# Block-attention residual on one core: where VectorE's row products take their factor from

## The chip, the cores and the metric

The kernel runs on one core of a Trainium2 chip. The metric is the device time of one execution in microseconds (us). The core has TensorE (PE in the profile; PEld is its weight load), VectorE (DVE), ScalarE (ACT), GpSimd (POOL) and SyncE (SP), whose queue issues almost all DMAs.

## What is computed

The input x is 8 x 512 x 1024 in float32, with a conditioning vector q and two 1024 x 1024 weights. For each batch entry, with H = 1024 and EPS = 1e-6:

```
block_repr = inputs.reshape(B, 8, 64, H).sum(axis=2)
keys = block_repr @ Wk.T;  keys = keys / sqrt(mean(keys^2) + EPS) * rms_weight
attn = softmax(keys @ q)
proj = (attn @ block_repr) @ Wo.T          # one row for each batch entry
y = inputs + proj
out = inputs + (y - mean(y)) / sqrt(var(y) + EPS) * ln_gamma + ln_beta
```

So every row of x needs the attention of its whole batch entry first, then a layer norm, and the original row is added at the end. Writing rs for a row's 1/std, mu for its mean and g for gamma, the result is y(1 + g rs) less a term of rank few: -proj - mu rs g + beta.

## The kernel before

**Tiling.** The 4096 rows are 32 "rows" of 128 partitions x 1024, numbered k = 0 to 31, two to a tile of 1 MB. The eight entries are worked on in three groups (`GROUPS`) of 2, 4 and 2 entries: k = 0 to 7, 8 to 23 and 24 to 31. Wk and Wo are loaded, turned on TensorE and kept.

**Attention of a group** (`attention`, L480). Sums over blocks go into `bs` on TensorE (L508); for tiles marked in `SUMS` with G or V, GpSimd or VectorE first adds the tile's two rows into `two` (L500), which halves TensorE's work. Then come keys, softmax, V (L534), and the projection spread over all partitions into a PSUM tile `pb` (L622). A bf16 table `tab` holds the rank-few term, cut into bf16 pieces by `split` (L411, L415).

**Unit and row** (`unit`, `pairs`, `pair`, `row`). For each row VectorE makes y = x + pb with its sum (L676) and ScalarE squares it (L683). A unit of 2 or 4 rows (`UNITS`) shares a `std` step on GpSimd (L692, L693) and a `sp` step (L715 to L719) that cuts mean x 1/std into three bf16 pieces in `stat`. Per tile TensorE turns these over into `pl` (L740), which ScalarE or VectorE (`TURN`) copies to `lt` (L745, L747). The matmul of `lt` with `tab` (L780) puts the rank-few term into a PSUM tile `C`. How the row is multiplied by (1 + g rs) is set by its letter in `KINDS`:

- A: ScalarE writes the factor to `A` (L776), GpSimd multiplies (L795), VectorE adds C (L826).
- P: as A, but TensorE adds the row into C by an identity matmul (L784) and ScalarE copies C out (L814).
- G: GpSimd multiplies by gamma into `A` (L797), TensorE puts the row into C (L784), VectorE does A x rs + C (L819).
- D: ScalarE writes the factor into C (L776), VectorE multiplies (L788) and, once TensorE has overwritten C, adds it (L826).
- E: VectorE alone: a reciprocal of rs (L790), (gamma + 1/rs) x row (L791, three operands in SBUF), then that x rs + C (L819).

Then the tile is stored (L763; the last tile in three parts, L758).

**Buffers and order.** `SLOTS` gives 13 x tiles, two `A`, and in PSUM three `big` tiles (4 KB each; used by `pb` and by every C) and two `s`. `A` and C are handed out in order of k. The order on each engine is a planner's: `Plan.order` takes, on each engine, the ready step with the lowest number in `RANK`, with assumed durations. The result is a fixed program for each engine's in-order queue. `EVAC` says which engine copies the turned weights and three small tiles of each group; where the plan leaves TensorE idle, filler matmuls (L859) are put in.

Of the kernel before, what the change touches and what calls it, by code (L numbers as in the profile page):

```python
# [20 lines left out]
SLOTS = {"x": 13, "A": 2, "big": 3, "s": 2, "lt": 2, "pr": 1, "tab": 2, "ts": 1, "blkT": 1,  # L21
# [3 lines left out]
SUMS = "PPVPGGPVPPPPPPPP"  # L25
EVAC = "ADAAAAAAAAADADADADAAAAADAAAD"
TURN = "ADDAAAAAAAAAAAAA"
FILL = (0.5, 0.3, 0.28)
KINDS = "GEDAAAPPGGEEAPAEPEPPGPPEEEEPEAAE"
UNITS = [[(1, "P"), (1, "P"), (1, "P"), (1, "P")], [(1, "P"), (1, "P"), (1, "P"), (1, "P"), (2, "P"), (2, "P")], [(2, "P"), (1, "P"), (1, "P")]]  # L30
# [6 lines left out]
5 33 6 31 28 16 21 30 34 26 25 7 0 11 1 4 9 3 10 2 14 13 17 19 12 15 46 55 67 18 68 37 70 79 175  # L37
205 93 214 20 22 27 24 23 8 38 40 45 63 35 39 29 36 41 43 44 62 66 74 52 73 51 65 53 72 64 78 77 92
86 89 90 100 49 60 69 71 76 42 47 32 48 57 61 56 58 54 50 75 81 80 85 91 82 95 83 87 98 96 94 99
106 101 104 111 117 121 124 109 107 113 154 122 132 133 136 115 108 137 153 131 140 145 161 134 135  # L40
127 156 142 146 150 167 155 162 173 172 160 171 158 177 181 119 128 114 123 176 143 163 159 165 179
130 184 174 187 203 189 192 138 88 110 116 152 191 197 195 185 208 196 220 231 188 217 207 232 216
235 97 102 105 59 120 84 118 103 125 170 129 139 141 144 148 147 151 149 168 169 166 190 180 183
182 164 178 186 126 112 157 198 204 201 234 226 202 206 200 212 223 265 199 233 218 211 242 250 225
213 276 248 270 221 237 193 194 274 280 241 260 239 254 268 249 258 275 289 215 224 228 251 294 298
259 278 264 312 266 295 272 308 245 256 300 307 229 257 222 243 299 219 244 283 293 316 291 284 310
271 263 319 227 240 292 303 287 297 269 279 330 338 320 317 311 343 334 329 350 315 335 340 345 321
318 322 351 324 342 352 327 357 333 348 354 358 305 314 313 353 288 309 210 285 370 383 360 363 378
355 367 376 349 423 365 369 381 391 361 368 374 379 380 387 398 328 373 331 404 209 230 236 238 255
247 261 253 267 246 252 302 296 273 306 304 301 281 277 282 290 286 262 325 341 323 337 388 396 336  # L50
346 356 364 326 339 344 371 372 386 392 397 332 347 395 400 401 394 414 399 407 382 409 393 390 362
410 412 417 420 366 385 377 384 389 405 403 406 436 416 424 402 411 418 415 428 359 408 375 413 419
421 425 426 422 438 429 434 427 430 431 432 437 435 433
# [117 lines left out]
def block_attn_resid_kernel(  # L171
# [25 lines left out]
    def flat(t):  # L197
        return t.rearrange("p a b -> p (a b)")
# [30 lines left out]
    ONES, MU = 12, 15  # L229
# [11 lines left out]
    b_w = Buf("A", [P, 5, P], F32, "wide")  # L241
# [6 lines left out]
    stat = {g: fixed([P, ROOM, 32], f"stat{g}", BF16) for g in sizes}  # L248
# [6 lines left out]
    inv = fixed([P, 4 * B], "inv")  # L255
# [35 lines left out]
    def c_small():  # L291
        pool.memset(eps_t, EPS)
        pool.memset(half_t[:, :1], -0.5)
        w = T(b_w)
        pool.tensor_copy(w[:, 0:4, :], row_of(GR).unsqueeze(2).to_broadcast([P, 4, P]))
        pool.tensor_copy(w[:, 4, :].rearrange("p (j m) -> p j m", j=4), row_of(0).unsqueeze(2).to_broadcast([P, 4, 32]))

# [45 lines left out]
    sums_ok = plan.add("c_sums", "DVE", 2.8, c_sums, [first])  # L343
# [3 lines left out]
    c_f = {g: plan.add(f"c_far{g}", "POOL", 0.3, lambda g=g: c_far(g), [sums_ok]) for g in sizes}  # L347
    c_p = {g: plan.add(f"c_pick{g}", "POOL", 2.4 if g < 4 else 2.8, lambda g=g: c_pick(g), [sums_ok]) for g in sizes}
    c_sp = {g: plan.add(f"c_spread{g}", "POOL", 0.5, lambda g=g: c_spread(g), [sums_ok]) for g in spread}
    c_st = {g: plan.add(f"c_stat{g}", "POOL", 1.0, lambda g=g: c_stat(g), [sums_ok]) for g in sizes}  # L350
# [68 lines left out]


# [242 lines left out]
    def unit(G, tiles, how):  # L663
        n, g = G["n"], G["g"]
        add = plan.add
        NU = RT * len(tiles)
        k0 = G["first"] + RT * tiles[0]
        sums = fixed([P, 5, NU], f"sum{k0}")
        at = lambda i: (xt[n, tiles[i // RT]][0], i % RT)
        X = lambda i: T(at(i)[0])[:, at(i)[1], :]  # L670
        sq, ys = [], []
        for i in range(NU):
            xb, ld = xt[n, tiles[i // RT]]
            y = add(
                f"y{k0 + i}", "DVE", 1.15,
                lambda i=i: nc.vector.scalar_tensor_tensor(  # L676
                    X(i), X(i), 1.0, flat(T(G["pb"])), ALU.mult, ALU.add, accum_out=sums[:, 0, i : i + 1]
                ), [ld, *G["pb_ok"]], [xb, G["pb"]],
            )
            ys.append(y)  # L680
            sq.append(add(
                f"sq{k0 + i}", "ACT", 1.27,
                lambda i=i: nc.scalar.activation(  # L683
                    junk, X(i), AF.Square, bias=sums[:, 0, i : i + 1], scale=-float(H),
                    accum_out=sums[:, 1, i : i + 1], saturate=False,
                ), [y], [xb],
            ))

        def std():
            v = sums  # L690
            if how == "P":
                pool.tensor_scalar(v[:, 2, :], v[:, 1, :], 1.0 / H**3, EPS, ALU.mult, ALU.add)  # L692
                pool.tensor_tensor(v[:, 4, :], v[:, 2, :], half_t[:, :NU], ALU.pow)  # L693
            else:
                nc.scalar.activation(v[:, 2, :], v[:, 1, :], AF.Ln, bias=eps_t, scale=1.0 / H**3)
                nc.scalar.activation(v[:, 4, :], v[:, 2, :], AF.Exp, scale=-0.5)

        if how == "P":
            rs = add(f"std{k0}", "POOL", {2: 0.96, 4: 1.28, 8: 1.9}[NU], std, [*sq, small], [])
        else:  # L700
            rs = add(f"std{k0}", "ACT", 0.45, std, [*sq, small], [])
        pairs(G, tiles, sums, ys, rs)

    def pairs(G, tiles, sums, ys, rs):
        n, g = G["n"], G["g"]
        NU = RT * len(tiles)
        k0 = G["first"] + RT * tiles[0]
        r0 = RT * tiles[0] % ROOM
        st = stat[g][:, r0 : r0 + NU, :]

        def pieces():

            at = lambda i: st[:, :, MU + 3 * i : MU + 3 * i + 3]
            wide = sums[:, 3, :].unsqueeze(2).to_broadcast([P, NU, 3])
            pool.tensor_tensor(sums[:, 3, :], sums[:, 0, :], sums[:, 4, :], ALU.mult)  # L715
            pool.tensor_copy(at(0), wide)  # L716
            pool.tensor_tensor(sums[:, 3, :], sums[:, 3, :], at(0)[:, :, 0], ALU.subtract)
            pool.tensor_copy(at(1), wide)
            pool.tensor_tensor(at(2), wide, at(1), ALU.subtract)  # L719

        before = [last_use.get((g, r0 + r)) for r in range(0, NU, RT)]
        a = plan.add(f"sp{k0}", "POOL", 1.36, pieces, [rs, c_st[g], *before], [])
        for t in tiles:
            r = RT * (t - tiles[0])
            last_use[g, r0 + r] = pair(G, t, sums, r, ys, rs, st[:, r : r + RT], a)

    def pair(G, t, sums, o, ys, rs, st, a):
# [23 lines left out]
        fin = [row(G, t, r, kinds[r], X, xb, sums[:, 4, o + r : o + r + 1], rs, lt, lt_ok, seen(r), C[r], A[r]) for r in range(RT)]  # L751
# [15 lines left out]
    def row(G, t, r, kind, X, xb, scale, rs, lt, lt_ok, seen, C, A):  # L767
# [18 lines left out]
        def product():  # L786
            if kind == "D":
                nc.vector.tensor_tensor(X(r), X(r), flat(T(C)), ALU.mult)  # L788
                return
            nc.vector.reciprocal(inv[:, k : k + 1], scale)  # L790
            nc.vector.scalar_tensor_tensor(X(r), gam, inv[:, k : k + 1], X(r), ALU.add, ALU.mult)  # L791
# [7 lines left out]
        elif kind == "D":  # L799
            a = add(f"A{k}", "ACT", 1.05, lambda: factor(flat(T(C))), [rs, gam_ok], [C])  # L800
            m = add(f"m{k}", "DVE", 1.15, product, [a], [C, xb])
            need.append(m)
        else:
            m = add(f"m{k}", "DVE", 1.3, product, [rs, gam_ok], [xb])
        c = add(f"C{k}", "PE", 0.38, lambda: outer(T(G["tab"]), kind != "G", kind != "P"), need, [C, lt, G["tab"]])
        if kind == "P":
            m = add(f"I{k}", "PE", 1.84, lambda: whole(False, True), [m, c], [C, xb])
        halves = k == S * B // P - 1
        ends = []
        for tag, cut in (("fa", slice(0, H // 2)), ("fb", slice(H // 2, H))) if halves else (("f", slice(0, H)),):  # L810
            if kind == "P":
# [4 lines left out]
            elif kind in "GE":  # L816
# [3 lines left out]
                        X(r)[:, cut], (at_A() if kind == "G" else X(r))[:, cut], scale, flat(T(C))[:, cut], ALU.mult, ALU.add  # L820
                    ), [c, m], [C, xb, *([A] if kind == "G" else [])],
# [74 lines left out]
```

## Time and profile before

| | |
|---|---|
| median of 3 runs | 149.99 us (149.7 to 150.47) |
| profiled execution: own time | 150.32 us |
| its span in the profile | 148.4 us, so 1.92 us lie around it |
| mean granted TensorE clock | 0.933 |
| busy: PE, DVE, ACT, POOL | 118.7, 103.5, 90.2, 94.3 us |
| first y of each group (L676) | 44.51, 70.43, 103.55 us |
| last VectorE instruction ends | 144.1 us |

Times within the execution count from the start of the span. A group of instructions is named by line, engine, operation and tiles, with its count, its busy time and the mean of one in ns. On VectorE one instruction often starts some 0.07 us before the one ahead is counted as finished; the "pitch", from start to start in an unbroken run, is what an instruction really takes of the engine.

### The profile page before, as it was taken

How to read it: one execution, taken by the hardware profiler on the slowest of the kernel's cores; microseconds unless marked ns; L12 is line 12 of the kernel's file. 1: busy time of each engine (PE TensorE's matmuls, PEld its weight loads, DVE VectorE, ACT ScalarE, POOL GpSimd, SP SyncE). 2: the span in 40 equal slices, each digit the busy share in tenths (PEclk: the TensorE clock that was granted, in tenths of full speed). 3: DMA queues.
4: the chain of work that ended last, by engine and by line, in shares of the span. 5: the costliest groups of instructions: out<-in, count | busy, mean ns of one | idle time of the engine just before them, and what ended most of it. 6: DMA issues, size and time to landing. Idle time of an engine off the chain costs nothing.

```text
span 148.4 us, 3151 instructions
## 1 busy us (share of the span) xinstructions
PE 118.7 (80%) x1222; PEld 72.5 (49%) x1222; DVE 103.5 (70%) x168; ACT 90.2 (61%) x148; POOL 94.3 (64%) x155
## 2 busy tenths in 40 slices
PE   4999959999988948999999869987978577299300
PEld 4999818888764513455543433553423123064100
DVE  4113003016439997687999999989999999946980
ACT  0319413565306968856799977899869698463200
POOL 8950000000057687899998689969999898997600
PEclk9999999999999996899999987999999999857965
DMA  5999999999999991549999207660706606660983
GB/s 168 402 430 422 417 387 407 402 413 421 419 422 415 417 382 42 221 119 338 426 395 404 86 0 287 283 283 0 287 0 283 283 0 283 283 249 35 377 329 143
DMA packets 7662, 42.15 MB, mean 284 GB/s; under 512 B 720, under 2 KB 736, under 8 KB 3680
## 3 DMA queue, kind: packets, MB, share of 16 engines
q1 hardware_dynamic: 7616, 41.95, 69.9%
q8 instruction: 9, 0.15, 0.4%
q14 instruction: 5, 0.04, 0.1%
q10 hardware_dynamic: 32, 0.02, 0.0%
HBM read 25.18 MB, written 16.78 MB: 283 GB/s over the span
## 4 chain that ended last, share of the span: by engine, by line
DVE 21%; PE 14%; issue 8%; ACT 8%; POOL 3%; DVEq 1%; POOLq 0%; ACTq 0%
DVE x L676 9%; DVE x L791 4%; ACT junk L683 4%; PE C L784 4%; PE keys L534 3%; DVE x L819 3%; PE V L534 3%; DVE x L826 2%; PE C L780 2%; ACT A L776 1%; PE pl L859 1%; POOL sum L693 1%; DVE ptab L415 1%; POOL stat L716 1%; PE pb L622 1%
## 5 line engine op out<-in xcount | busy, mean ns | idle before, releaser
L683 ACT ACTIVATE junk<-x,sum 128x1024 fp8e5<-128x1024 f32 x32 | 36.7, 1148 | 10.2 <-DVE x L676 8.3
L795 POOL TENSOR_TENSOR x<-x,A 128x1024 f32<-128x1024 f32 x16 | 38.5, 2429 | 1.0 <-ACT A L776 1.0
L676 DVE SCALAR_TENSOR_TENSOR x<-x,pb 128x1024 f32<-128x1024 f32 x32 | 37.6, 1214 | 0.9 <-PE pb L622 0.8
L784 PE MATMUL C<-x,ident 128*128 128x512 f32 x52 | 26.6, 642 | 0.5 <-POOL x L795 0.3
L500 POOL TENSOR_TENSOR two<-x 128x1024 f32<-128x1024 f32 x2 | 4.7, 2362 | 33.7 <-DMA x<-in_x_dram 32.9
L776 ACT ACTIVATE A<-gam,sum 128x1024 f32<-128x1024 f32 x16 | 18.2, 1147 | 2.7 <-POOL x L795 1.3
L791 DVE SCALAR_TENSOR_TENSOR x<-gam,inv,x 128x1024 f32<-128x1024 f32 x11 | 17.8, 1621 | 0.6
L443 PE MATMUL pt<-ident,w 128*128 128x128 f32 x128 | 15.6, 275 | 1.1 <-DMA w<-in_L_cond_Wk_dram 0.4
L784 PEld LDWEIGHTS C<-x,ident 128*128 128x128 f32 x52 | 9.6, 200 | 12.3 <-issue 9.0
L819 DVE SCALAR_TENSOR_TENSOR x<-x,sum,C 128x1024 f32<-128x1024 f32 (+1 forms) x12 | 14.1, 1186 | 2.0 <-PE C L780 1.9
L443 PEld LDWEIGHTS pt<-ident,w 128*128 128x128 f32 x128 | 13.9, 141 | 2.9 <-issue 1.4
L534 PE MATMUL keys<-wkT,blkT 128*32 128x128 f32 (+1 forms) x256 | 14.5, 372 | 0.0
L693 POOL TENSOR_TENSOR sum<-sum,half_t 128x2 f32<-128x2 f32 (+1 forms) x13 | 13.0, 1001 | 1.1
L508 PE MATMUL bs<-x,blk 128*32 128x256 f32 x192 | 12.0, 382 | 1.9 <-DMA x<-in_x_dram 1.9
L780 PE MATMUL C<-tab,lt 32*128 32x512 bf16 x64 | 8.5, 404 | 4.7 <-DVE x L819 2.0
L534 PE MATMUL V<-woT,blkT 128*32 128x128 f32 (+1 forms) x256 | 11.8, 328 | 0.0
L814 ACT COPY x<-C 128x1024 f32<-128x1024 f32 x9 | 8.9, 1004 | 4.0 <-POOL sum L693 3.6
L826 DVE TENSOR_TENSOR x<-x,C 128x1024 f32<-128x1024 f32 x8 | 9.6, 1214 | 1.2 <-POOL stat L716 1.2
L797 POOL TENSOR_TENSOR A<-x,gam 128x1024 f32<-128x1024 f32 x4 | 9.5, 2374 | 1.1 <-ACT junk L683 1.1
L534 PEld LDWEIGHTS keys<-wkT,blkT 128*32 128x32 f32 x256 | 7.7, 122 | 4.6 <-issue 2.9
L740 PE MATMUL pl<-identb,stat 128*32 128x128 bf16 x64 | 4.0, 237 | 6.3 <-POOL stat L719 4.3
L508 PEld LDWEIGHTS bs<-x,blk 128*32 128x32 f32 x192 | 5.5, 109 | 7.0 <-DMA x<-in_x_dram 2.8
(116 smaller groups left out, 168.6 us busy)
## 6 DMA issues: line engine op xcount, KB each, us to landing
x<-in_x_dram SPq DMA_DIRECT2D x16, 1024.0 KB, 10.5
out_dram<-x SPq DMA_DIRECT2D x15, 1024.0 KB, 3.9
w<-in_L_cond_Wk_dram SPq DMA_DIRECT2D x3, 1024.0 KB, 7.8
w<-in_L_cond_Wo_dram SPq DMA_DIRECT2D x3, 1024.0 KB, 15.7
w<-in_L_cond_Wk_dram SPq DMA_DIRECT2D x2, 512.0 KB, 3.2
w<-in_L_cond_Wo_dram SPq DMA_DIRECT2D x2, 512.0 KB, 16.5
out_dram<-x SPq DMA_DIRECT2D x2, 256.0 KB, 2.0
out_dram<-x SPq DMA_DIRECT2D x1, 512.0 KB, 2.6
```

Of the source, the lines that this page charges most:

```text
L443: nc.tensor.transpose(T(pt)[:, c, r * P : (r + 1) * P], T(sb)[:, r, bass.ts(4 * h4 + c, P)], ident)
L508: nc.tensor.matmul(T(bs)[32 * j : 32 * j + 32, :], blk[g], part()[:, bass.ts(j, QU)], start=(t == 0 and r == 0), stop=(t == nt - 1 and r = ...
L534: nc.tensor.matmul(dst[32 * j : 32 * j + 32, lo:hi], T(blkT)[:, c % 2, c // 2, :], wT[:, c, j * QU + lo : j * QU + hi], start=(c == 0), st ...
L676: lambda i=i: nc.vector.scalar_tensor_tensor(X(i), X(i), 1.0, flat(T(G["pb"])), ALU.mult, ALU.add, accum_out=sums[:, 0, i : i + 1]), [ld, ...
L683: lambda i=i: nc.scalar.activation(junk, X(i), AF.Square, bias=sums[:, 0, i : i + 1], scale=-float(H), accum_out=sums[:, 1, i : i + 1], sa ...
L693: pool.tensor_tensor(v[:, 4, :], v[:, 2, :], half_t[:, :NU], ALU.pow)
L776: nc.scalar.activation(out, gam, AF.Identity, bias=1.0, scale=scale)
L784: nc.tensor.matmul(T(C)[:, h, :], ident, X(r)[:, bass.ts(h, 2 * QU)], start=start, stop=stop)
L791: nc.vector.scalar_tensor_tensor(X(r), gam, inv[:, k : k + 1], X(r), ALU.add, ALU.mult)
L795: m = add(f"m{k}", "POOL", 2.37, lambda: pool.tensor_tensor(X(r), X(r), at_A(), ALU.mult), [a], [A, xb])
L819: lambda cut=cut: nc.vector.scalar_tensor_tensor(X(r)[:, cut], (at_A() if kind == "G" else X(r))[:, cut], scale, flat(T(C))[:, cut], ALU.m ...
L826: lambda cut=cut: nc.vector.tensor_tensor(X(r)[:, cut], X(r)[:, cut], flat(T(C))[:, cut], ALU.add),
```

## The change

No row is of kind E any more. Two kinds are new. In kind F TensorE writes g x rs into C by a matmul of `lt` with a new constant table `rise` (gamma rows in bf16 pieces) and VectorE multiplies the row by (C + 1); the rest is as in D. In kind R the product is F's and the end is P's (identity matmul, copy by ScalarE). So that `lt` can carry rs, rs too is cut in three pieces: the `sp` step does both numbers at once, with six instructions in place of five. `A` gets a third buffer. The kinds by group, the tiles added up ahead, the engines of copies, the units and the whole order change as well:

| | before | after |
|---|---|---|
| kinds, k = 0 to 7 | GEDAAAPP | GFADAAAP |
| k = 8 to 23 | GGEEAPAE PEPPGPPE | GGFFRGPA PFPAFFGP |
| k = 24 to 31 | EEEPEAAE | APDFPAFA |
| SUMS by tile | PPVP GGPVPPPP PPPP | PPGP GPPGPGPP GPPP |
| rows per unit | 2 2 2 2, 2 2 2 2 4 4, 4 2 2 | 2 2 2 2, 2 2 4 4 4, 4 4 |
| weight copies by DVE | 3 | 7 |
| `blkT`, `bss` by group | ADA, AAA | DAA, DAA |
| `lt` copies by DVE (tiles) | 1, 2 | 0, 1, 13, 15 |

```diff
-SLOTS = {"x": 13, "A": 2, "big": 3, "s": 2, "lt": 2, "pr": 1, "tab": 2, "ts": 1, "blkT": 1,
+SLOTS = {"x": 13, "A": 3, "big": 3, "s": 2, "lt": 2, "pr": 1, "tab": 2, "ts": 1, "blkT": 1,
...
-    stat = {g: fixed([P, ROOM, 32], f"stat{g}", BF16) for g in sizes}
+    stat = {g: fixed([P, ROOM, 33], f"stat{g}", BF16) for g in sizes}
+    rise = fixed([P, 2 * QU], "rise", BF16)
...
+        pool.memset(w[:, 6:8, :], 0.0)
+        for k in range(2):
+            v = w[:, 6 + k, :].rearrange("p (r i m) -> p r i m", r=2, i=2)
+            spot(v, RS, 8, k, GR)
...
+    b_r = buf("s", [P, 2, QU], "prise")
+    def rise_rows():
+        for k in range(2):
+            nc.tensor.matmul(T(b_r)[:, k, :], T(b_w)[:, 6 + k, :], gbq, start=True, stop=True)
+    pr_ok = plan.add("prise", "PE", 1.1, rise_rows, [vec, small], [b_r, b_w])
+    ri_ok = split(b_r, lambda: rise, "r", [pr_ok], [])
...
-            pool.tensor_tensor(sums[:, 3, :], sums[:, 0, :], sums[:, 4, :], ALU.mult)
-            pool.tensor_copy(at(0), wide)
-            pool.tensor_tensor(sums[:, 3, :], sums[:, 3, :], at(0)[:, :, 0], ALU.subtract)
-            pool.tensor_copy(at(1), wide)
-            pool.tensor_tensor(at(2), wide, at(1), ALU.subtract)
+            pool.tensor_tensor(own_rs(sums, 0), sums[:, 0, :], own_rs(sums, 1), ALU.mult)
+            pool.tensor_copy(at(0, 3), wide(3))
+            pool.tensor_tensor(cut(5), cut(3), at(0, 1)[:, :, :, 0], ALU.subtract)
+            pool.tensor_copy(at(3, 3), wide(5))
+            pool.tensor_tensor(cut(5), cut(5), at(3, 1)[:, :, :, 0], ALU.subtract)
+            pool.tensor_copy(at(6, 3), wide(5))
...
-                return
-            nc.vector.reciprocal(inv[:, k : k + 1], scale)
-            nc.vector.scalar_tensor_tensor(X(r), gam, inv[:, k : k + 1], X(r), ALU.add, ALU.mult)
+            else:
+                nc.vector.scalar_tensor_tensor(X(r), flat(T(C)), 1.0, X(r), ALU.add, ALU.mult)
...
+            else:
+                a = add(f"B{k}", "PE", 0.4, lambda: outer(rise), [lt_ok, ri_ok], [C, lt])
             m = add(f"m{k}", "DVE", 1.15, product, [a], [C, xb])
             need.append(m)
-        else:
-            m = add(f"m{k}", "DVE", 1.3, product, [rs, gam_ok], [xb])
...
-        if kind == "P":
+        if kind in "PR":
             m = add(f"I{k}", "PE", 1.84, lambda: whole(False, True), [m, c], [C, xb])
```

All numbers of `RANK` are new, and some of the planner's assumed durations.

## The prediction on record

> **What bounds the kernel now.** First the table of busy time by stretches. Its columns are the length, then PE, PEld, DVE, ACT and POOL busy with counts, the granted clock, the DMA share and GB/s:
>
> ```profile
> 44.50:70.40 25.90, 22.50 (x286) 11.17 (x286) 22.54 (x38) 18.97 (x32) 21.59 (x35) 0.93 0.70 276
> 70.40:144.10 73.70, 56.85 (x410) 27.11 (x410) 69.20 (x98) 54.86 (x93) 62.16 (x79) 0.92 0.56 228
> ```
>
> From 70.4 us, where the second group's first y starts, to the end of the last VectorE instruction, VectorE is busy for 69.2 of 73.7 us; DMA has slack. GpSimd has 62.2, yet little of the rest is idle: its small instructions leave some 0.07 us between them. Before 70.4 the second group's attention sets the pace (x tiles landing, sums, keys, V, all on DMA and TensorE), so a faster VectorE there mostly waits longer. I count gains from 70.4 on.
>
> Next the groups of instructions with forms kept apart (busy us and mean ns after the bar, then idle before):
>
> ```profile
> L795 POOL TENSOR_TENSOR x<-x,A 128x1024 f32<-128x1024 f32 x16 | 38.5, 2429 | 1.0 <-ACT A L776 1.0
> L676 DVE SCALAR_TENSOR_TENSOR x<-x,pb 128x1024 f32<-128x1024 f32 x32 | 37.6, 1214 | 0.9 <-PE pb L622 0.8
> L791 DVE SCALAR_TENSOR_TENSOR x<-gam,inv,x 128x1024 f32<-128x1024 f32 x11 | 17.8, 1621 | 0.6
> L819 DVE SCALAR_TENSOR_TENSOR x<-x,sum,C 128x1024 f32<-128x1024 f32 x10 | 12.7, 1274 | 1.9 <-PE C L780 1.9
> L826 DVE TENSOR_TENSOR x<-x,C 128x1024 f32<-128x1024 f32 x8 | 9.6, 1214 | 1.2 <-POOL stat L716 1.2
> ```
>
> The E product (L791) has a mean of 1621 ns, but its shortest is 1283 and its median 1285. So the eleven hold 17.8 - 11 x 1.285 = 3.7 us of something else. The timeline says what; DVE's lines, then POOL's (start, duration):
>
> ```profile
> 104.88 3.14 DVE L791 SCALAR_TENSOR_TENSOR x<-gam,inv,x 128x1024 f32<-128x1024 f32 x1
> ...
> 126.91 1.28 DVE L791 SCALAR_TENSOR_TENSOR x<-gam,inv,x 128x1024 f32<-128x1024 f32 x1
> ```
> ```profile
> 102.25 7.99 POOL L795 TENSOR_TENSOR x<-x,A 128x1024 f32<-128x1024 f32 x3
> ...
> 125.10 1.60 POOL L693 TENSOR_TENSOR sum<-sum,half_t 128x2 f32<-128x2 f32 x1
> 126.78 0.19 POOL L715 TENSOR_TENSOR sum<-sum 128x2 f32<-128x2 f32 x1
> 127.04 1.21 POOL L716 CAST stat<-sum 128x6 bf16<-128x6 f32 x1
> 128.33 0.20 POOL L717 TENSOR_TENSOR sum<-sum,stat 128x2 f32<-128x2 f32 x1
> ```
>
> Where an E product meets GpSimd, one waits for the other. At 104.88 it takes 3.14 us beside three GpSimd products that take 7.99 where three others take 7.05. At 127.04 a copy of six numbers takes 1.21 us, elsewhere 0.20, as the E product from 126.91 runs. Nine GpSimd instructions are stretched so (starts 53.12, 84.93, 100.53, 102.25, 113.89, 122.44, 125.10, 127.04, 134.06), each beside an L791: 1.03 + 1.07 + 1.01 + 0.94 + 0.99 + 0.99 + 0.89 + 1.01 + 0.91 = 8.8 us of GpSimd's time, 7.8 of it after 70.4. No y (L676, all 1206 to 1220 ns) and no L826 (1207 to 1221) is stretched, though GpSimd multiplies beside most: they read one tensor in SBUF and one in PSUM. The E product reads two in SBUF.
>
> **VectorE, from 70.4 on.** Pitches: L791 with its reciprocal 0.19 + 1.20 (84.67 to 86.06), L819 1.20, y 1.14, L826 1.13. Rows 8 to 31 before: ten E at 2.59 = 25.9, with the 3.7 us of waiting 29.6; three G at 1.2 = 3.6; four A at 1.13 = 4.5; P nothing: 37.7. After: an F product is y's instruction with the operands the other way about, so I take y's 1.14, between 1.13 (L826) and 1.20 (L819); F = 1.14 + 1.13. Seven F 15.9, R 1.1, D 2.3, four G 4.8, five A 5.7: 29.8. That is 7.9 less; two `lt` copies more (L747, pitch 0.2) give 0.4 back: **-7.5 us**. At 1.20 a product, 0.5 more.
>
> A rule of the Trainium skill speaks against it: "VectorE: DVE Perf Modes", section on the TRN2 errata, gives a fixed 120 cycles to an instruction from PSUM and 58 to one from SBUF. By it each product would be 65 ns longer than L791, the eight 0.5 us. In the rows the one with PSUM is 71 ns shorter (1214 against 1285); the rows decide.
>
> The last operand is the SBUF one in F, the PSUM one in y. Of that form the trace has L562 (keys in PSUM, then qw): 423 to 425 ns all three times, at 63.48 inside a run of GpSimd products, at 34.19 with GpSimd idle. So F should not wait for GpSimd.
>
> **GpSimd, from 69.6 on.** It runs to 140.40, 70.8 us. Before: two products left of group 0, 4.7; eleven for A and P at 2.35, 25.9; three for G, 7.1; six units of two rows at 2.4 and three of four at 2.65 (the seven instructions with their gaps), 22.4; stretched 7.8; 2.9 idle. After: 4.7; eleven again (6 P, 5 A) 25.9; four G 9.4; units longer by one small instruction, 0.27: two at 2.67 and five at 2.92, 19.9; one `two` for the third group 2.4; idle kept 2.9: 65.2, which is **5.6 us less**, to an end near 134.8.
>
> **TensorE** gets eight B pairs (nearest L780, 0.40: 3.2 us) and one identity matmul more (1.9), less half a tile's sums (0.5): +4.6 on 56.9, of which 6.4 are fillers. ScalarE gets one factor more and one copy less. Both stay below VectorE.
>
> **Before 70.4.** The table `rise` costs TensorE 1.0 us (nearest L400, eight in 1.97), ScalarE two casts of 0.57, VectorE two L415 of 0.74, GpSimd three small instructions of 0.2 to 0.3. Loads keep DMA full until 55 us, ScalarE and VectorE are idle for over half of the first 40, GpSimd from 10 to 42: hidden. If the cover on TensorE fails, 1.0 us. Four weight copies more on VectorE (1.22 each) hide too. A gain may lie here: the sums that finish the second group's `bs` start at 55.29, queued behind `pl`, which waited 1.67 us for a stretched `sp`. I value the part at nothing, between -1.0 and +1.0.
>
> **New waits.** An E product waited for `std` alone. F waits for `sp`, `pl`, `lt` and B. Behind it on VectorE's queue stand other rows, for whom the stores wait. Exposed, B, C and the hops between engines cost some 0.4 + 0.4 + 0.3 = 1.1 us a row. While y's are left the planner has other work to put there. I take 1.5 us in all, for the end of the last group, between 0 and 8 x 1.1 = 8.8. Units of four rows hold up the first row by two squarings (1.27 each), covered likewise. The third `A` is worth up to the 1.0 us that L795 waited for L776; I give it nothing.
>
> **Sum.** VectorE ends 7.5 - 1.5 = 6.0 us sooner, at 138.1. GpSimd's 134.8 with a last addition in halves (2 x 0.65) gives 136.1 for the end: second, close behind. The stores' 4.3 us after the last VectorE instruction stay. The profiled 150.32 becomes 144.3; the median lies 0.33 below the profiled run, so **144.0**.
>
> **Rivals.**
>
> *The waits eat part of it.* A C tile of kind F is held for B, product, C and addition, some 3.8 us with hops, against 2.0 for E (C, addition, hops), and there are three, one of them `pb` while y's are made. With half of the 8.8 us exposed, 4.4 in place of 1.5, the time is 147; with three quarters, 6.6, it is 149. For it: TensorE's queue is in order, a B that stands for a tile holds the other rows. Against it: 7 x 1.8 us more holding is small beside three tiles over 66 us.
>
> *Slower: the chain of B, product and C decides.* If every F and R row stands exposed, 8.8 us, at the point where `lt` and B come no sooner than VectorE reaches the product, VectorE's 7.5 are gone: 150.0 + 1.3 = 151.3. From 7 of 8 rows on it is no gain. For it: VectorE waited 1.9 us for C at 132.4 already. Against it: that was in the tail, with stretched `std` and `sp` ahead.
>
> *It doesn't do what it says:* F products meet GpSimd after all, because their second operand is in SBUF. Then VectorE keeps 3.7 and GpSimd 7.8; GpSimd's work rises by 2.2 and it ends near 142.6, with the halved addition 143.9 against 144.1 now: about 149.8. L562 speaks against it, though it is short.
>
> *More:* no new wait comes (1.5), half of the tail's two VectorE waits (1.9 and 1.2) goes, and the second group starts 1.0 sooner: 144.0 - 1.5 - 1.5 - 1.0 = 140.
>
> **Chances.** Forecast (142 to 146.5) 0.62; part eaten (146.5 to 149.2) 0.15; more 0.07; doesn't do what it says 0.05; slower 0.11. A measurement tells half a per cent, 0.75 us, from no change: faster by more 0.84, within 0.05, slower 0.11. For 8 in 10 I leave out the slower case and the ends of the gain: 141.0 to 149.5.
>
> **What would show it.** In the profile after: the F product near 1.21 us, never stretched; every small GpSimd instruction near 0.2, `std`'s 0.7 to 1.0; VectorE over 90% busy until the last group's y's are made, at a sum about 7 us smaller; last VectorE instruction near 138. I am wrong if idle time on VectorE, ended by PE (B or C), passes 4 us after the second group's start, if the groups' first y's come later than 70.4 and 103.5, or if GpSimd runs on past 136.

## The result and the profile after

The changed kernel takes **145.36 us** in the median of four runs (142.9, 143.74, 146.98, 147.12), the kernel before 150.11 beside it; the ratio is 0.955 [0.948, 0.961]. A second time (below) it took 143.77 in the median of six, beside 150.81: 0.953 [0.947, 0.958]. Ratios leave out the runs of a kernel that took over 1.5% longer than its fastest (above the two of 147 us, at a granted clock of 0.92 to 0.93 against 0.957 and 0.967), so a ratio need not equal the quotient of two medians.

The profiled execution took 142.9 us: a span of 141.0 at a mean granted clock of 0.967. First the busy time of each engine in the whole span:

```profile
PE 117.0 (83%) x1206; PEld 68.6 (49%) x1206; DVE 101.5 (72%) x164; ACT 86.6 (61%) x143; POOL 95.2 (68%) x159
```

VectorE (103.5 before) has lost 2.0 us in all and GpSimd (94.3) has gained 0.9. So the 7.4 us that the span is shorter cannot be seen in the totals. The table by stretches shows it, with the columns of the prediction's first table; the second line is again from the second group's first y to the end of the last VectorE instruction:

```profile
44.50:70.40 25.90, 21.77 (x285) 11.43 (x284) 22.73 (x37) 19.19 (x34) 21.30 (x39) 1.00 0.84 338
69.52:135.67 66.15, 57.15 (x402) 25.28 (x402) 63.40 (x90) 54.16 (x90) 56.53 (x74) 0.97 0.56 230
```

That stretch was 73.7 us and is 66.15. VectorE's busy time in it fell from 69.2 to 63.4 (5.8 us), its idle time from 4.5 to 2.75 (1.75). GpSimd's busy time fell from 62.2 to 56.5 and its last instruction ends at 132.23, not 140.40. The groups of instructions with forms kept apart, as before:

```profile
L813 POOL TENSOR_TENSOR x<-x,A 128x1024 f32<-128x1024 f32 x16 | 37.6, 2368 | 1.6 <-ACT A L795 1.6
L689 DVE SCALAR_TENSOR_TENSOR x<-x,pb 128x1024 f32<-128x1024 f32 x32 | 37.8, 1215 | 2.1 <-PE pb L635 2.1
L809 DVE SCALAR_TENSOR_TENSOR x<-C,x 128x1024 f32<-128x1024 f32 x9 | 10.9, 1220 | 0.8 <-PE C L799 0.8
L845 DVE TENSOR_TENSOR x<-x,C 128x1024 f32<-128x1024 f32 x18 | 21.6, 1215 | 1.7 <-POOL x L813 1.3 <-POOL sum L733 0.3
```

L809 is the new product, L813 GpSimd's (L795 before), L845 the last addition (L826), L689 the y (L676). The product's mean is 1220 ns, and no single one is longer than 1.23 us. GpSimd's large product has gone from 2429 to 2368 ns. What a small GpSimd instruction does beside a product is seen in the timeline (start, duration); VectorE's line, then GpSimd's:

```profile
115.83 2.35 DVE L809 SCALAR_TENSOR_TENSOR x<-C,x 128x1024 f32<-128x1024 f32 x2
```
```profile
115.62 0.20 POOL L737 TENSOR_TENSOR sum<-sum,stat 128x8 f32<-128x8 f32 x1
115.89 0.23 POOL L738 CAST stat<-sum 128x24 bf16<-128x24 f32 x1
...
125.24 6.99 POOL L813 TENSOR_TENSOR x<-x,A 128x1024 f32<-128x1024 f32 x3 [0.98 <-ACT A L795]
```

The copy of 24 numbers at 115.89 lies wholly under a product and takes 0.23 us; its like, on six numbers, took 1.21 at 127.04 before. Three large GpSimd products beside a product of VectorE (125.26, 1.22 us) take 6.99; before, at 102.25, 7.99.

What VectorE waits for in that stretch (total, times, longest):

```profile
DVE x L689 <- PE pb L635: 1.2, 1, 1.2
DVE x L845 <- POOL x L813: 1.0, 1, 1.0
DVE x L809 <- PE C L799: 0.8, 1, 0.8
DVE x L807 <- ACT C L795: 0.3, 1, 0.3
DVE x L845 <- POOL sum L733: 0.3, 1, 0.3
```

The first ends as the stretch begins. Of the others only L809's 0.8 us is a wait of the kind that the change brings: a product that waits for B. This profile is of the fastest run; in that of experiment 5, the same kernel at 143.65 us, it is more:

```profile
DVE x L809 <- PE C L799: 1.9, 2, 1.2
```

### The profile page after: what moved, and what is told of

Its sections match the earlier page's. It is cut to its first block, busy times and chain, and to the rows that moved or that the text cites. A ratio compares the mean times of both kernels' runs of the same rounds, so it can differ in the third digit from the quotient of the medians.

```text
span 141.0 us, 3124 instructions
## 1 busy us (share of the span) xinstructions
PE 117.0 (83%) x1206; PEld 68.6 (49%) x1206; DVE 101.5 (72%) x164; ACT 86.6 (61%) x143; POOL 95.2 (68%) x159
## 3 DMA queue, kind: packets, MB, share of 16 engines
q1 hardware_dynamic: 7616, 41.95, 73.7%
## 4 chain that ended last, share of the span: by engine, by line
DVE 25%; DMA 24%; POOL 16%; PE 14%; issue 8%; ACT 6%; SPq 2%; DVEq 1%; POOLq 0%; ACTq 0%
DMA w<-in_L_cond_Wo_dram 12%; DVE x L689 12%; POOL x L813 8%; DMA x<-in_x_dram 7%; PE C L803 7%; DVE x L845 5%; DMA wq<-in_cond_dram 4%; ACT junk L696 4%; DVE x L809 3%; POOL A L815 3%; PE V L547 2%; SPq L390 2%; ACT x L833 2%; DVE x L838 2%; POOL sum L706 2%
## 5 line engine op out<-in xcount | busy, mean ns | idle before, releaser
L689 DVE SCALAR_TENSOR_TENSOR x<-x,pb 128x1024 f32<-128x1024 f32 x32 | 37.8, 1215 | 2.1 <-PE pb L635 2.1
L813 POOL TENSOR_TENSOR x<-x,A 128x1024 f32<-128x1024 f32 x16 | 37.6, 2368 | 1.6 <-ACT A L795 1.6
L513 POOL TENSOR_TENSOR two<-x 128x1024 f32<-128x1024 f32 x5 | 11.8, 2363 | 25.1 <-PE pc L586 18.1
L845 DVE TENSOR_TENSOR x<-x,C 128x1024 f32<-128x1024 f32 (+1 forms) x20 | 22.8, 1162 | 1.8 <-POOL x L813 1.3
L795 ACT ACTIVATE A<-gam,sum 128x1024 f32<-128x1024 f32 x16 | 18.1, 1145 | 1.0 <-POOL x L813 0.6
L815 POOL TENSOR_TENSOR A<-x,gam 128x1024 f32<-128x1024 f32 x5 | 11.8, 2380 | 2.4 <-DVE x L689 2.3
L465 ACT COPY wkT<-pt 128x1024 f32<-128x1024 f32 x6 | 6.1, 1012 | 9.5 <-PE pt L456 9.5
L799 PEld LDWEIGHTS <-lt 32*128 32x128 bf16 x82 | 3.6, 91 | 16.5 <-issue 12.8
L809 DVE SCALAR_TENSOR_TENSOR x<-C,x 128x1024 f32<-128x1024 f32 x9 | 10.9, 1220 | 0.8 <-PE C L799 0.8
L547 PE MATMUL keys<-wkT,blkT 128*32 128x128 f32 (+1 forms) x256 | 11.4, 327 | 0.0
L706 POOL TENSOR_TENSOR sum<-sum,half_t 128x2 f32<-128x2 f32 (+1 forms) x11 | 9.3, 843 | 0.9
L547 PEld LDWEIGHTS V<-woT,blkT 128*32 128x32 f32 x256 | 7.2, 110 | 3.4 <-issue 0.5
L416 ACT CAST ts<-ptab 128x512 bf16<-128x512 f32 x6 | 3.4, 574 | 8.7 <-PE ptab L666 8.5
```

The lines of the kernel that those rows point to most:

```text
L547: nc.tensor.matmul(dst[32 * j : 32 * j + 32, lo:hi], T(blkT)[:, c % 2, c // 2, :], wT[:, c, j * QU + lo : j * QU + hi], start=(c == 0), st ...
L689: lambda i=i: nc.vector.scalar_tensor_tensor(X(i), X(i), 1.0, flat(T(G["pb"])), ALU.mult, ALU.add, accum_out=sums[:, 0, i : i + 1]), [ld, ...
L706: pool.tensor_tensor(own_rs(v, 1), v[:, 2, :], half_t[:, :NU], ALU.pow)
L795: nc.scalar.activation(out, gam, AF.Identity, bias=1.0, scale=scale)
L799: nc.tensor.matmul(T(C)[:, h, :], T(lt)[blocks[h], :], rhs[blocks[h], :], start=start, stop=stop)
L809: nc.vector.scalar_tensor_tensor(X(r), flat(T(C)), 1.0, X(r), ALU.add, ALU.mult)
```

## The experiments

Two theories stood at the start. **Theory 1:** the gain is the end of the mutual waiting of VectorE's E product, with its two tensors in SBUF, and GpSimd. **Theory 2:** it is something else that changed along with it: fewer rows on VectorE, the third buffer, the new order, a better clock. Times are medians; ratios are against the kernel before, run beside each, with 95% intervals.

**1. The waiting put back.** In the changed kernel the nine products read gamma rows from SBUF in place of C. Left out: their 1/std.

```diff
-nc.vector.scalar_tensor_tensor(X(r), flat(T(C)), 1.0, X(r), ALU.add, ALU.mult)
+nc.vector.scalar_tensor_tensor(X(r), gam, 1.0, X(r), ALU.add, ALU.mult)
```

> The changed kernel, its plan and order untouched, with one operand other: the nine products of kinds F and R read the gamma rows in SBUF where they read C in PSUM. So they multiply by gamma + 1 and leave out 1/std, which changes the result of those nine rows; B is still computed and not read. Theory 1 (the gain comes from VectorE no longer reading two tensors from SBUF beside GpSimd): products of 1.21 us alone, several stretched to 1.5 to 3, some six to nine GpSimd instructions stretched by about 1.0 each, and 3 to 6 us more than the changed kernel. Theory 2 (the gain comes from the new mix and order of steps): within 0.7 us of the changed kernel.

Measured: 149.26 us; 0.9925 [0.989, 0.996]. With everything else in the program the same, 5.5 of the some 7 us are lost again. The group of products in this kernel, then the timeline at the place that was shown for the changed kernel (VectorE's line, then GpSimd's):

```profile
L809 DVE SCALAR_TENSOR_TENSOR x<-gam,x 128x1024 f32<-128x1024 f32 x9 | 12.4, 1389 | 0.0
```
```profile
119.83 2.36 DVE L809 SCALAR_TENSOR_TENSOR x<-gam,x 128x1024 f32<-128x1024 f32 x2
```
```profile
119.91 1.21 POOL L737 TENSOR_TENSOR sum<-sum,stat 128x8 f32<-128x8 f32 x1
121.18 1.10 POOL L738 CAST stat<-sum 128x24 bf16<-128x24 f32 x1
```

The same two instructions beside the same two products: 1.21 and 1.10 us where they took 0.20 and 0.23. VectorE's products lose only 1.5 us in all (12.4 - 10.9); GpSimd's busy time rises from 95.2 to 102.6. The price is paid mostly by the other engine, in instructions of 0.2 us that are stretched by 0.9 to 1.0 us, most of a product. Theory 1 holds for this kernel.

**2. The old product in the new order.** The eight F rows are done the E way (reciprocal, three operands, then x rs + C) at the places of the changed kernel.

```diff
+nc.vector.reciprocal(inv[:, k : k + 1], scale)
+nc.vector.scalar_tensor_tensor(X(r), gam, inv[:, k : k + 1], X(r), ALU.add, ALU.mult)
```

> The changed kernel and its order, but the eight F rows computed as E rows were: reciprocal, product of three operands in SBUF, and at the end x times rs plus C (R stays). VectorE has 8 x (0.19 + 0.06 + 0.07) = 2.6 us more of its own. Theory 1: that, and the waits of the run with the SBUF operand on top: 5 to 8 us more than the changed kernel, which is all of the gain. Theory 2: at most the 2.6 us, and about 146 us.

Measured: 153.59 us in the median of six; the runs scatter from 150.69 to 154.60, so there is no ratio and the size is worth little. Even the lowest is 6.9 us above the changed kernel's 143.77, more than VectorE's own 2.6, and level with the kernel before: the gain is gone. Whether the E product does worse in this order than in its own isn't shown. In the profile (of a run of 154.0 us) the product's group has a mean of 1839 ns and GpSimd is busy for 101.6 us.

```profile
L814 DVE SCALAR_TENSOR_TENSOR x<-gam,inv,x 128x1024 f32<-128x1024 f32 x8 | 14.7, 1839 | 0.4
```

**3. The waiting taken away in the kernel before.** Old kinds, old order, old buffers; only the E product reads one tensor. Left out: gamma in those rows.

```diff
-nc.vector.scalar_tensor_tensor(X(r), gam, inv[:, k : k + 1], X(r), ALU.add, ALU.mult)
+nc.vector.tensor_scalar(X(r), X(r), inv[:, k : k + 1], 1.0, ALU.mult, ALU.add, accum_out=inv[:, k : k + 1])
```

> The kernel before, its plan and order untouched, with the E product done on one tensor: x times 1/rs plus 1, with an accumulator output, in place of (gamma + 1/rs) times x. This changes the eleven E rows' result. Theory 1: no GpSimd instruction is stretched, GpSimd gets back up to 8.8 us and VectorE 3.7, and since the order was written for products that don't wait, 3 to 6 us less than the kernel before. Theory 2: less than 1 us.

Measured: 143.30 us; 0.9555 [0.951, 0.960]. This is as much as the whole change gains, from one instruction. The product's group, GpSimd's large product, and the stretch from the second group's first y on:

```profile
L791 DVE TENSOR_SCALAR_CACHE_REDUCE x<-x,inv 128x1024 f32<-128x1024 f32 x11 | 14.1, 1279 | 0.6
...
L795 POOL TENSOR_TENSOR x<-x,A 128x1024 f32<-128x1024 f32 x16 | 37.6, 2375 | 2.4 <-ACT A L776 2.4
```
```profile
69.67:136.29 66.62, 54.63 (x410) 26.16 (x410) 65.48 (x109) 54.90 (x93) 55.36 (x80) 0.97 0.63 254
```

VectorE is busy for 65.5 us in place of 69.2: 3.7 less, the waiting that the prediction had read out of L791's mean. GpSimd is busy for 85.8 us in all in place of 94.3: 8.5 less, where the prediction counted 8.8. And VectorE's idle time in that stretch goes from 4.5 to 1.1, since what it waited for at the end (C behind a stretched `std` and `sp`; GpSimd's `stat`) now comes in time. 3.7 + 3.4 is the gain of 7.1 in that stretch. The three waits of 1.9, 1.2 and 0.7 us that VectorE had there are down to one:

```profile
DVE junkd L562 <- ACT junk L558: 0.3, 1, 0.3
```

**4. The new kind alone.** In the kernel before, every E becomes F; its mix, units, copies, two `A` buffers and order otherwise stay.

```diff
-KINDS = "GEDAAAPPGGEEAPAEPEPPGPPEEEEPEAAE"
+KINDS = "GFDAAAPPGGFFAPAFPFPPGPPFFFFPFAAF"
```

> The new kind alone: every E of the kernel before is made F, with the three pieces of 1/std, and the other kinds, the tiles summed ahead, the units, the engines of copies and the two A buffers stay as before. The ranks are those of before by name; B, and lt, pl and sp where an F row needs them sooner, go just ahead of the product. Theory 1: faster than before by 3 to 6 us. Theory 2: within 1 us of before, or slower, since the order is not fitted to the new kind.

Measured: 155.70 us; 1.035 [1.029, 1.041]: slower, as theory 2 allowed. The waiting is gone here as well (GpSimd's large product 2367 ns, GpSimd busy for 89.3 us), yet 12 us are lost against experiment 3. The second group's first y comes at 76.49 us, not 70.43, and from 69.5 us on VectorE's longest waits are all on TensorE:

```profile
DVE x L861 <- PE C L815: 2.8, 1, 2.8
DVE x L705 <- PE pb L651: 2.8, 2, 1.4
DVE pr L642 <- PE V L563: 2.7, 1, 2.7
```

So F by itself is not a gain. It ends the mutual waiting and asks for something in return.

**5. The changed kernel again**, for the spread of its first four runs.

> The changed kernel itself, beside the runs below on one chip. Its four times so far lie in two heaps, 142.9 and 143.7 us at a granted clock of 0.967 and 0.957, and 147.0 and 147.1 at 0.924 and 0.926. Expected: 143 to 144 where the clock is 0.955 or more, 147 where it is 0.93 or less; a ratio to the kernel before of 0.955 to 0.975.

Measured: 143.77 us; 0.953 [0.947, 0.958], six runs from 143.06 to 145.55. The clock does not sort them well: 143.19 came at 0.947, 145.55 at 0.952.

**6. The changed kernel with two `A` buffers**, in its own order.

```diff
-SLOTS = {"x": 13, "A": 3, ...
+SLOTS = {"x": 13, "A": 2, ...
```

> The changed kernel with two A buffers in place of three; the planner makes its order again from the same ranks. If the third buffer carries part of the gain, GpSimd waits for ScalarE's factor (L795) or for VectorE's reading of A longer than the 1.6 us of the changed kernel, and the time is 1 to 4 us above it. If it doesn't, within 0.7 us.

Measured: 164.50 us; 1.093 [1.087, 1.099]. The third group's first y comes at 128.35 us (97.61). The largest waits, GpSimd's from 44 us on and then VectorE's from 69.5 on:

```profile
POOL sum L705 <- ACT junk L696: 21.9, 4, 15.6
```
```profile
DVE x L845 <- PE C L799: 10.8, 6, 4.1
```

I had valued the third buffer at nothing, and expected 4 us here at most. Taken at its word this run says 20 us; experiments 10 and 12 ask whether it may be taken so.

**7. One half of F's price.** In the kernel before, the E product takes gamma from C, which TensorE fills just ahead by a matmul of ones with gamma's pieces. So it reads one tensor in SBUF and holds a C from there on, as F does, but needs neither `lt` nor `sp` first.

```diff
+nc.tensor.matmul(T(C)[:, h, :], onesb[blocks[h], :], rise[blocks[h], :], start=True, stop=True)
...
-nc.vector.scalar_tensor_tensor(X(r), gam, inv[:, k : k + 1], X(r), ALU.add, ALU.mult)
+nc.vector.scalar_tensor_tensor(X(r), flat(T(C)), inv[:, k : k + 1], X(r), ALU.add, ALU.mult)
```

> The kernel before with its kinds, units, buffers and order; only the E product takes gamma from PSUM: TensorE writes the gamma rows into C by a matmul of ones, at a rank just ahead of the product, and VectorE computes (C + 1/rs) times x; then as before. It has no need of lt, pl and sp ahead of the product, unlike the kind-alone run (155.7 us), but holds a C tile as long. It computes the reference. Theory 1a (lt and sp ahead of the product cost the kind-alone run its gain): 143 to 146 us. Theory 1b (holding the C tile from the product to the addition, with three tiles in order of k, costs it): 150 us or more, with VectorE and TensorE waiting for C.

Measured: 147.85 us; 0.980 [0.974, 0.985], between experiments 3 and 4, and between the two theories' times.

```profile
L824 DVE SCALAR_TENSOR_TENSOR x<-C,inv,x 128x1024 f32<-128x1024 f32 x11 | 14.1, 1284 | 2.5 <-PE C L840 0.7 <-DVE inv L823 0.5 <-PE C L813 0.5
```
```profile
69.39:140.90 71.51, 60.61 (x452) 30.99 (x452) 65.64 (x98) 55.17 (x93) 55.11 (x79) 0.97 0.56 232
```

VectorE's work is that of experiment 3 (65.6 us), so the product is not stretched, though like L791 it has three operands: one of the two tensors now comes from PSUM. With experiment 1, where two tensors in SBUF and a constant were stretched, this says that the second SBUF tensor counts, and not the number of operands. What differs is the idle time, 5.9 us for 1.1. By the ratios, holding C (and the matmuls that fill it) costs 0.980 - 0.956 = 2.4% or 3.6 us in the old order. The rest of the way to experiment 4, 5.5% or 8.3 us, is what comes with needing `sp`, `pl` and `lt` ahead of the product, with F's other steps and with an order that was not fitted to them (experiment 11).

**8. The filler matmuls taken out** of the changed kernel, for the clock.

```diff
-FILL = (0.5, 0.3, 0.28)
+FILL = (0.5, 0.3, 1e9)
```

> The changed kernel without the filler matmuls, at the start and later, nothing else moved. If the gain, or part of it, comes from the higher granted clock (0.967 in the profile after, 0.933 before), the clock falls to 0.93 or lower and the time rises to 146 to 150 us. If the clock is a result of shorter gaps on TensorE, and no cause, within 1 us of the changed kernel.

Measured: 143.61 us; 0.951 [0.945, 0.956], with a clock of 0.958 in the profile: the same as with them. As the clock did not fall, this run can't say what a lower one would cost. Single runs can: the kernel before took 149.79 us at a granted clock of 0.966 (beside experiment 9), the changed kernel 143.19 at 0.947 (experiment 5). The gain is not one of the clock.

**9. The third buffer alone**, in the kernel before and its order.

```diff
-SLOTS = {"x": 13, "A": 2, ...
+SLOTS = {"x": 13, "A": 3, ...
```

> The kernel before with three A buffers and nothing else; same ranks, the planner may place the steps that were waiting for a buffer sooner. If the third buffer is a gain by itself: 1 to 3 us less than the kernel before. If it serves only the new order: within 0.8 us of it, since L795 waited for L776 for 1.0 us in all.

Measured: 153.60 us; 1.017 [1.010, 1.024]. One buffer more makes the old kernel slower by some 1.7%, which neither case had expected. Its order was found for two; that this is the cause was not tested here.

**10. Two buffers with one `two` step less.** As experiment 6, but the tile of the third group that GpSimd had added up into `two` (which takes an `A`) is summed by TensorE alone.

```diff
-SUMS = "PPGPGPPGPGPPGPPP"
+SUMS = "PPGPGPPGPGPPPPPP"
```

> The changed kernel with two A buffers, as in the run of 164.5 us, but the rows of the third group's first tile are not added up ahead on GpSimd: TensorE sums both. There GpSimd did that sum at 72.2 us; then two G rows held both buffers, and the third group's first y came at 128.4 in place of 97.6. If it is the step 'two' that must hold a buffer while the G rows need theirs: back to 144 to 148 us. If G, P and A rows themselves need three: still 155 us or more.

Measured: 161.01 us; 1.070 [1.065, 1.076]. Little better; the `two` step of the third group is not what made experiment 6 slow. By the expectation's terms the rows themselves would need three buffers; experiment 12 asks that with another order.

**11. The new kind alone, with an order fitted to it.** Experiment 4 with new numbers in `RANK`, found by a random search for the planner's earliest end.

> The kind-alone run (155.7 us: every E made F, mix of kinds, units, copies and two buffers as before), with new ranks: some 60,000 random changes of the old ones were tried and the order with the earliest planned end kept. If only the order was unfitted: 143 to 146 us, as the changed kernel. If the new mix is needed as well, because F rows want more of TensorE and of the C tiles than E rows did: 147 to 151, between the two.

Measured: 149.99 us in the median of six; the ratio, 0.981 [0.974, 0.988], rests on two runs, 147.25 and 147.46. In the profile, which is of a run of 149.9 us, the second group's first y comes at 73.74, and VectorE still waits for C, five times:

```profile
DVE x L861 <- PE C L815: 5.9, 5, 2.3
```

By these two runs, order gives back 5.4 of the 8 points (1.035 to 0.981) that lie between experiment 4 and the changed kernel. The other 2.8 points, some 4 us, belong to what is still different, which is the mix of kinds (eight F and an R in place of eleven F; more A, G and D, fewer P), units, copies, tile sums and the third buffer, or to a better order that the search did not find. This was not separated.

**12. Two buffers, with an order fitted to two.** The changed kernel as in experiment 6, its order searched anew in the same way.

> The changed kernel with two A buffers, as in the run of 164.5 us, but with ranks fitted to two buffers (30,000 random changes of the ranks, the order with the earliest planned end kept). If the rows of the new mix need three buffers: 152 us or more. If only the order needed them: 144 to 148 us, so the third buffer itself is worth 0 to 4 us and the rest of the 20 us was an order made for three buffers and run with two.

Measured: 145.34 us; 0.960 [0.954, 0.966]. The changed kernel's ratios are 0.953 and 0.955: once the order suits two buffers, the third is worth 0.5 to 0.7%, some 1 us, and the intervals overlap. Nearly all of the 20 us of experiment 6 was the price of an order made for three and run with two.

No version ran faster than the changed kernel by more than the intervals: experiment 8 equals it, and so does experiment 3, which leaves gamma out.

## Why the prediction was right

The direction, the mechanism and the size held: 144.0 was forecast, which is 0.960 of the 149.99 us before, and 0.955 and 0.953 were measured. By its steps, against the profiled execution (144.3 forecast, 142.9 measured, the fastest of its four runs):

- **F is never stretched, and neither is GpSimd beside it.** Right: 1220 ns against 1.21. The argument from L562, which was short, holds for 1024 columns. Experiments 1 and 3 show it as the cause: put back, 5.5 us are lost; taken away in the old kernel, the whole gain is there. The Trainium skill, "SBUF — State Buffer", section "Who interferes with whom", says that a VectorE instruction with two SBUF inputs contends with a GpSimd instruction that reads SBUF, and one with at most one SBUF input, outside the modes that the page calls 2-port, does not. All these runs agree with it: on 1024 columns no VectorE instruction of a row with at most one tensor in SBUF took more than 1285 ns, while products of two took up to 3140 (before).
- **VectorE's work from the second group's first y: -7.5 us.** Measured -5.8. One row of the first group is now added behind that first y, 1.1 us that the count of rows 8 to 31 did not hold. The 0.6 that is left I did not trace; busy time and pitches differ by about as much.
- **New waits: +1.5 us.** This is the term that was mis-sized: VectorE's idle time in that stretch fell by 1.75. For F's own waits the 1.5 was fair, 0.8 us here and 1.9 in experiment 5's profile; but the old waits at the end (1.9 for C, 1.2 for `stat`, 0.7 for ScalarE) went. The prediction had this case among its rivals ("more") and gave it 0.07. What it had missed is seen in experiment 3: the stretched GpSimd instructions cost VectorE a further 3.4 us as idle time, and that leaves with them.
- **Sum from the second group's first y:** -5.8 - 1.75 = -7.55, where -6.0 was forecast; 1.5 more.
- **Before 70.4: nothing.** The second group's first y came at 69.52, 0.9 sooner. In the bounds; the gain that "may lie here" was real, and it belongs to the mutual waiting too: with the waiting put back the y comes at 70.47 (experiment 1), with it taken away in the kernel before at 69.67 (experiment 3).
- **The stores' 4.3 us unchanged.** Wrong by 1.0: from the last VectorE instruction (135.67) to the end of the span it is 5.3. The last stores took 3.3 to 3.5 us to land, before 2.0 to 2.6. The table of stretches shows the DMA engines busier from 125 to 130 us, 0.90 in place of 0.57 (before, then after). At the same distance from its own end, 132.4 to 137.4 us, the kernel before has 0.30:

```profile
125.00:130.00 5.00, 1.26 (x17) 0.61 (x13) 4.96 (x6) 2.86 (x6) 4.55 (x8) 0.86 0.57 236
```
```profile
125.00:130.00 5.00, 3.77 (x21) 1.54 (x20) 3.99 (x6) 3.31 (x5) 4.76 (x3) 0.82 0.90 374
```

  Rows that finish closer together are also stored closer together. That these longer stores come of it was not tested.
- **GpSimd ends near 134.8.** 132.23: not the bound. **TensorE's +4.6 are hidden.** VectorE waited for it 0.8 us after the first y, so hidden is right. The 4.6 can't be read off: TensorE is busy for 57.15 us in the stretch, 56.85 before, at a clock of 0.97 for 0.92.
- **Third `A`: nothing.** Some 1 us, at the upper bound, against an order that suits two, and not clear of the intervals.

144.3 - 1.5 - 0.9 + 1.0 = 142.9. That it came so close is in part luck: in the stretch 1.7 us too much was taken off for work and 3.25 too little for waiting, and the late stores took back what the early start gave.

**The rival of the slower side** (B, product and C as the chain that decides) was a real mechanism: in the old order it is worth more than the mutual waiting (experiment 4, 1.035), and experiment 7 shows holding C, with the matmuls that fill it, as some 3.6 us of it. My price of 8.8 us was too low for that order (experiment 4 lies 12 us above experiment 3); my 1.5 held in the new one. What separates them is order, and perhaps mix: with an order found for it F gains some 2% (experiment 11), with fewer F rows and what else was changed beside them 4.5 to 4.7%. The reason that I gave against the milder rival, in which the waits eat part of the gain ("small beside three tiles over 66 us"), would have been wrong for the old order. That the new order avoids the waits could not be read from the profile before; in that the prediction was lucky.

**What stays open.** How the last 4 us divide between the mix, the units, the copies, the tile sums and the quality of the order: none was tried by itself. Which of `sp`, `pl`, `lt` and the steps' places makes most of the 8.3 us between experiments 7 and 4.

## What to carry to other kernels

When a group's mean lies well over its shortest instruction, look in the timeline at what runs beside the long ones, and count the loss on both engines: here the product's own 3.7 us were half of what VectorE got back in experiment 3; the other 3.4 were waits behind GpSimd, which got back 8.5. A VectorE instruction with one of its two tensors in PSUM did not meet GpSimd in any run here; but a PSUM tile that is filled early and held long had a price of its own (some 3.6 us in experiment 7), and how much of it is paid depends on the order. An order found for one set of buffers can mislead about another set: fit it anew before a buffer is judged (20 us became some 1).

## What was not expected of the hardware

- A GpSimd instruction on 4 to 24 numbers a partition, 0.20 to 0.23 us by itself, takes 1.06 to 1.24 beside a VectorE product of two SBUF tensors (experiment 1). The engines' losses are very unequal: in experiment 1 VectorE lost 1.5 us, GpSimd 7.4.
- The prediction took the 71 ns between L791 (1285) and y (1214) as a sign that PSUM costs nothing. It was the scalar: with a scalar from SBUF the product takes 1284 ns with its tensor from PSUM (experiment 7) and 1285 from SBUF; with a constant 1220 ns from PSUM and, where nothing stretches it, 1.22 us from SBUF (experiment 1). So the source made no difference that these rows show, and the scalar some 65 ns. The extra 65 ns for PSUM, an estimate that the prediction worked out from the Trainium skill ("VectorE: DVE Perf Modes", section on the TRN2 errata), appears in neither pair; the measurement decides.
- Filler matmuls, which take 6.4 us of TensorE from 70.4 us on in the kernel before, bought nothing in the changed one (0.951 without, 0.953 with).
